# Three of the first seven weight tiles move from one load queue to the other

## The chip, the cores and the metric

The kernel runs on one core of one Trainium2 chip. The metric is the device time of one execution in microseconds (us). The engines are TensorE (PE in the rows, with PEld for its weight loads), VectorE (DVE), ScalarE (ACT), GpSimd (POOL) and SyncE (SP). SP, ScalarE and GpSimd each issue DMAs on a queue of their own; in the rows these issues stand as SPq, ACTq and POOLq.

## The reference

Two layers of a relational graph attention network over 3125 nodes of 768 features, 53125 edges and 3 relations, then a residual sum and a layer norm:

```python
xr = jnp.einsum('nd,rdf->rnf', x, W)          # W: 3 x 768 x 768
qi = xr[etype, dst] @ q; kj = xr[etype, src] @ k
alpha = leaky_relu(qi + kj, 0.2)
a = segment_softmax(alpha, dst)               # by destination node
out = segment_sum(a[:, :, None] * oj.reshape(-1, heads, out_ch), dst) + b
...
h = elu(layer(x, W1, q1, k1, b1)); out = layer(h, W2, q2, k2, b2)
return layernorm(x + out)
```

The first layer has four heads, the second one. The edges are sorted by destination.

## The kernel before, in words

The kernel has a preparation, which takes some 120 us, and three phases, which take the rest. Every matmul of fp32 data is made of a high part (a cast) and a low part (the difference); that is what the names H and L stand for (`wH`, `wL`, `tH`, `tL`).

The order of the work is written out by hand: within the manual schedule each engine does its instructions in the order in which the Python code issues them.

The preparation goes through the 18 tiles of W1, each 128 rows of 768 values (384 KB), two at a time. In `weights_kq`, `turn(m)` transposes tiles 2m and 2m+1 on TensorE (line 263), ScalarE makes the high part of each tile (line 303), VectorE or GpSimd the low part (line 304; VectorE for every third tile), ScalarE and VectorE split the transposed tiles (lines 273 and 274). `product` multiplies them by k and q (line 285), `place` writes the result into `wk` (lines 319 to 325). After `turn(m)` come `product(m-1)` and `place(m-2)`.

The tiles come in by `Buffers`: seven buffers of the tile `share` are filled at once, and each one that is freed (after its low part) takes the next tile of the list, W1's first, then x's blocks. All these loads stand on SP's queue (lines 178 and 181).

Beside the weights runs `prepare`, a generator of which `more(1)` does one step after each group. Its first step loads the three edge arrays dst, src and edge type as 125 rows of 425 int32 values (line 191, ScalarE's queue). Its second step scales dst on VectorE (line 208), stores it to a DRAM array `ed_d` (line 205) and fills the margins of `ed_d` and `dr_d` with constants, in four small-grained stores (lines 211 and 212); all five stores stand on GpSimd's queue, ahead of the low parts that GpSimd makes. A later step joins src and edge type (line 216, VectorE).

The tile framework deals out eight completion semaphores in turn to the loads of SP's and ScalarE's queues, in the order of the program. An issue whose semaphore still belongs to a load under way waits for that load.

Of the kernel before, what the change touches and what calls it, by code (L numbers as in the profile page):

```python
# [20 lines left out]
P = 128  # L21
# [33 lines left out]
def kernel(  # L55
# [19 lines left out]
    nc = tc.nc  # L75
# [7 lines left out]
    l1, l2 = layers  # L83
# [67 lines left out]
    class Buffers:  # L151
# [20 lines left out]
        def go(self):  # L172
            while self.waiting and self.spare:
                key = self.waiting.pop(0)
                self.at[key] = self.spare.pop(0)
                kind, i = key
                if kind == "W":
                    nc.sync.dma_start(self[key], l1["W"].rearrange("r (t p) f -> (r t) p f", p=P)[i])
                elif kind == "x":
                    n = min(P, N - i * P)  # L180
                    nc.sync.dma_start(self[key][:n], x[i * P:i * P + n, :])
# [305 lines left out]
    def a_load(pre, b):  # L487
        s = a_st[b] = {}
        r0 = start(b, regs)
        s["T"] = pre.tile([3 * (SL + 1), P], F32, name="T", bufs=2)  # L490
        nc.sync.dma_start(s["T"], at(ed_d, 0, 0, [[LL, 3], [P, SL + 1], [1, P]], r0))
# [755 lines left out]
    with tc.manual_schedule():  # L1247
        with tc.tile_pool(name="share", bufs=1) as pool:
            share = [pool.tile([P, RW], F32, name=f"share{i}") for i in range(9)]

            two = pall.rearrange("p b j h -> p (b j h)")
            xbs = [t[:, :D] for t in share] + [two[:, i * D:(i + 1) * D] for i in range(2)]
            with tc.tile_pool(name="wbuf", bufs=1) as wbuf:
                wH = wbuf.tile([P, R * DT, D + 2], F32R, name="wH")
                wL = wbuf.tile([P, R * DT, D + 2], F32R, name="wL")
                with tc.tile_pool(name="pre", bufs=1) as pre:
                    qq = pre.tile([P, NB, H1, R], F32, name="qq")
                    with tc.tile_pool(name="work0", bufs=1) as work, tc.tile_pool(
                        name="psum0", bufs=1, space=PSUM
                    ) as psum:  # L1260

                        bank = psum.tile([P, 512], F32, name="bank")
                        bits = prepare(work, bank, share[8], share[6].bitcast(BF))

                        def more(n):
                            for _ in range(n):
                                next(bits, None)

                        buf = Buffers()
                        buf.go()  # L1270
                        kqr = work.tile([P, DT, 2, H1], F32, name="kqr", bufs=1)
                        for s, name in ((0, "k"), (1, "q")):
                            nc.scalar.dma_start(kqr[:, :, s, :], l1[name].rearrange("(t p) h -> p t h", p=P))
                        more(1)
                        wk, kqs = (work.tile([P, DT, P], F32R, name=n) for n in ("wk", "kqs"))

                        def edges_ready():
                            more(100)
                            a_load(pre, 0)

                        turns = nodes_kq(buf, pre, work, psum, bank, wk, kqs, wH, wL, qq, more, edges_ready)
                        weights_kq(buf, work, psum, bank, kqr, wk, kqs, wH, wL, next(turns), more)
                        next(turns)
                    with tc.tile_pool(name="work1", bufs=1) as work, tc.tile_pool(
                        name="psum1", bufs=1, space=PSUM
                    ) as psum:
                        phase1(pre, work, psum, wH, wL, qq)
                with tc.tile_pool(name="work2", bufs=1) as work, tc.tile_pool(name="psum2", bufs=1, space=PSUM) as psum:
                    phase2(work, psum, wH, wL)
            with tc.tile_pool(name="work3", bufs=1) as work, tc.tile_pool(name="psum3", bufs=1, space=PSUM) as psum:  # L1290
                phase3(work, psum)
# [538 lines left out]
```

## Time and profile before

| | us |
|---|---|
| median of 3 runs | 2750.47 |
| lowest and highest | 2748.6, 2752.66 |
| the profiled execution's own time | 2741.27 |
| its span | 2739.5 |
| TensorE busy | 2054.5 (75%) |
| GpSimd busy | 1322.5 (48%) |
| VectorE busy | 1195.6 (44%) |
| ScalarE busy | 369.7 (13%) |

The rows of the profile come from one execution. Its times are counted from the start of the span; the execution's own time lies a little above the span, and this execution was some 9 us faster than the median of the timed runs. A row of the timeline has the start, the length, the engine, the line, the operation, what is written and read, and in brackets how long the engine was idle before it and what released it. Line numbers are those of the kernel before.

### The profile page before, as it was taken

The page shows a single profiled execution, that of the slowest core. Times are in us where ns is not written, and L with a number is a line of the kernel's source. Part 1 is how long each engine was busy: PE and PEld are TensorE (multiplying, and loading weights), DVE is VectorE, ACT ScalarE, POOL GpSimd, SP SyncE. Part 2 cuts the span into 40 slices and gives each one's busy share as a digit, 9 for nine tenths or more (in the row PEclk, how much of TensorE's full clock was granted, in tenths as well). Part 3 has the DMA queues.
Part 4 walks back from the last instruction along what each step waited for, and adds up shares of the span by engine and source line. Part 5 has one row for each costly group of instructions (what it writes and reads, how often), then busy time and mean ns, then how long its engine had stood idle before and what let it go on. Part 6 is the DMA issues. An engine that isn't in the chain of part 4 may idle for free.

```text
span 2739.5 us, 41906 instructions
## 1 busy us (share of the span) xinstructions
PE 2054.5 (75%) x15027; PEld 1606.6 (59%) x15027; DVE 1195.6 (44%) x4159; ACT 369.7 (13%) x658; POOL 1322.5 (48%) x1326
## 2 busy tenths in 40 slices
PE   7867888777776767888888898889936566565655
PEld 6756676667665645777677777767723232333323
DVE  6423333333332245445544554455424545444444
ACT  5301111111111000101110111111100111111111
POOL 3355555454543454444444434443255656566561
PEclk9967888888887878999999999999966777676777
DMA  7533333333332467666665656665577888877781
GB/s 193 142 95 120 114 114 114 113 106 115 103 108 99 143 213 244 198 201 203 203 200 187 214 185 211 192 212 191 175 271 246 272 267 267 276 253 259 251 262 61
DMA packets 156844, 506.31 MB, mean 185 GB/s; under 512 B 43875, under 2 KB 57069, under 8 KB 156628
## 3 DMA queue, kind: packets, MB, share of 16 engines
q0 software_dynamic: 81904, 331.52, 39.8%
q1 hardware_dynamic: 62926, 156.02, 16.1%
q10 hardware_dynamic: 11798, 16.00, 1.9%
q8 instruction: 122, 2.00, 0.3%
q14 instruction: 94, 0.77, 0.1%
HBM read 412.55 MB, written 95.69 MB: 186 GB/s over the span
## 4 chain that ended last, share of the span: by engine, by line
PE 52%; issue 17%; another core or an unknown queue 12%; DVE 11%; POOL 3%; DMA 3%; ACT 1%; POOLq 0%; ACTq 0%; DVEq 0%; SPq 0%
PE po L931 15%; PE po L698 14%; PE acc L875 9%; PE acc L1126 8%; DVE selp L853 3%; POOL G L462 2%; DMA G<-ftab,ridx 1%; PE bank L285 1%; DVE y L888 1%; PE bc L1033 1%; PE pt L263 1%; PE pt L906 1%; PE po L395 1%; DVE selp L1112 1%
## 5 line engine op out<-in xcount | busy, mean ns | idle before, releaser
L462 POOL DMA_INDIRECT kt<-kt,ridx x374 | 393.6, 1052 | 387.7 <-DVE lim L557 266.3
L698 PE MATMUL po<-wH,xT 128*128 128x384 f32 x1584 | 498.5, 382 | 107.5 <-issue 67.0
L931 PE MATMUL po<-wH,hT 128*128 128x386 f32 (+1 forms) x1800 | 514.7, 361 | 31.7 <-issue 27.3
L462 POOL DMA_INDIRECT G<-ftab,ridx x374 | 372.9, 997 | 242.2 <-PE acc L1126 110.4
L1126 PE MATMUL acc<-G,selp 128*32 128x386 f32 x2488 | 343.2, 621 | 102.6 <-DVE selp L1112 79.9
L698 PEld LDWEIGHTS po<-wH,xT 128*128 128x128 f32 x1584 | 331.2, 215 | 145.0 <-issue 92.0
L931 PEld LDWEIGHTS po<-wH,hT 128*128 128x128 f32 x1800 | 353.0, 202 | 67.3 <-issue 61.9
L853 DVE TENSOR_SCALAR selp<-frow,fdl,pall 128x32 f32<-128x32 f32 (+1 forms) x1688 | 380.3, 309 | 20.1 <-remote 17.3
L462 POOL DMA_INDIRECT share<-ftab,ridx x239 | 238.4, 997 | 299.7 <-PE acc L875 223.4
L931 PE MATMUL po<-wL,hT 128*128 128x386 f32 (+1 forms) x900 | 321.9, 358 | 14.4 <-issue 14.4
L698 PE MATMUL po<-wL,xT 128*128 128x384 f32 x792 | 296.2, 374 | 36.3 <-issue 35.8
L1126 PEld LDWEIGHTS acc<-G,selp 128*32 128x32 f32 x2488 | 190.6, 132 | 217.4 <-DVE selp L1112 107.0
L875 PE MATMUL acc<-share,selp 128*32 128x193 f32 x3208 | 229.6, 335 | 35.0 <-issue 31.4
L462 POOL DMA_INDIRECT g<-ftab,ridx x135 | 134.7, 998 | 191.9 <-PE acc L875 146.5
L698 PEld LDWEIGHTS po<-wL,xT 128*128 128x128 f32 x792 | 170.3, 215 | 48.3 <-issue 48.1
L875 PEld LDWEIGHTS acc<-share,selp 128*32 128x32 f32 x3208 | 131.0, 111 | 107.7 <-issue 77.5
L931 PEld LDWEIGHTS po<-wL,hT 128*128 128x128 f32 x900 | 182.4, 203 | 17.7 <-issue 17.4
L939 ACT COPY r<-po 128x386 f32<-128x386 f32 (+1 forms) x150 | 72.2, 481 | 834.5 <-PE po L931 621.4
L875 PE MATMUL acc<-g,selp 128*32 128x193 f32 x1768 | 139.4, 332 | 18.6 <-issue 15.7
L713 ACT COPY share<-po 128x384 f32<-128x384 f32 x144 | 67.1, 478 | 594.3 <-remote 260.6
L943 DVE COPY q<-po 128x1 f32<-128x1 f32 x75 | 11.6, 155 | 275.8 <-ACT r L939 275.7
L1039 DVE TENSOR_SCALAR sT<-bc,cols 128x512 bf16<-128x512 f32 (+1 forms) x125 | 83.4, 668 | 108.1 <-PE bc L1033 87.4
(245 smaller groups left out, 1986.0 us busy)
## 6 DMA issues: line engine op xcount, KB each, us to landing
ftab<-share SPq DMA_DIRECT2D x75, 386.0 KB
ftab<-r SPq DMA_DIRECT2D x75, 386.0 KB
share<-in_L_gnn_W_dram SPq DMA_DIRECT2D x36, 384.0 KB
w_d<-w2hl SPq DMA_DIRECT2D x18, 768.0 KB
sT<-dr_d SPq DMA_DIRECT2D x25, 544.0 KB
share<-in_x_dram SPq DMA_DIRECT2D x25, 384.0 KB
xb_d<-share SPq DMA_DIRECT2D x25, 384.0 KB
xr<-in_x_dram SPq DMA_DIRECT2D x23, 384.0 KB
```

The lines of the kernel that those rows point to most:

```text
L263: T.transpose(pt[:, f, c * P:(c + 1) * P], a[:, (2 * i + f) * P:(2 * i + f + 1) * P], ident)
L285: T.matmul(to, a[:, 2 * i + f, :], t[:, f, :w], start=(n == 0), stop=(n == 2 * DT - 1))
L395: T.matmul(po[g][:, :HALF], a[:, t % 2, :], w[:, r * DT + t, c * HALF:(c + 1) * HALF], start=(t == 0 and n == 0), stop=(t == DT - 1 and n ...
L462: return G.indirect_dma_start(out=to, out_offset=None, in_=tab, in_offset=_index(i[:, j:j + 1]), bounds_check=NP * R - 1, oob_is_err=False)
L698: m = T.matmul(po[:, :HALF], xT[:, s, t, :], w[:, i, sl], start=(n == 0), stop=(n == 3 * DT - 1))
L713: S.copy(to, po[:, :HALF].rearrange("p (h f) -> p h f", h=2))
L853: V.tensor_scalar(sel[:, h, :hi - lo], row[:, lo:hi], dl[:, b, j:j + 1], pall[:, b, j, h:h + 1], op0=ALU.is_equal, op1=ALU.mult)
L875: T.matmul(acc[32 * t:32 * t + 32, h // 2, c], sel[:, h, 32 * (t - WINDOW[i][0]):][:, :32], g[:, h * CW:(h + 1) * CW], start=(i == u[0] an ...
L931: T.matmul(po[:, :wd], hT[:, k, t, :], w[:, r * DT + t, sl], start=(t == 0 and n == 0), stop=(t == DT - 1 and n == 2))
L939: S.copy(o[:, c * HW:c * HW + wd], po[:, :wd])
L1039: V.tensor_scalar(s["sT"][:, 4 * i * P:4 * i * P + n], bc[:, :n], cols[:, b:b + 1], None, op0=ALU.is_equal)
L1126: T.matmul(acc[32 * t:32 * t + 32, c, :HW], st[b, j][:, 32 * (t - WINDOW[j][0]):][:, :32], gs[:, (base(b) + j) % NG, c * HW:(c + 1) * HW], ...
```

## The change

Tiles 1, 3 and 5 of W1 are issued on ScalarE's queue; all others stay with SP. `buf.go()`, which issues the first seven tiles, moves behind the issues of k and q. So on ScalarE's queue the order is k, q, three tiles, dst, src, edge type.

```diff
                 if kind == "W":
-                    nc.sync.dma_start(self[key], l1["W"].rearrange("r (t p) f -> (r t) p f", p=P)[i])
+                    (nc.scalar if i in (1, 3, 5) else nc.sync).dma_start(self[key], l1["W"].rearrange("r (t p) f -> (r t) p f", p=P)[i])
...
                         buf = Buffers()
-                        buf.go()
                         kqr = work.tile([P, DT, 2, H1], F32, name="kqr", bufs=1)
                         for s, name in ((0, "k"), (1, "q")):
                             nc.scalar.dma_start(kqr[:, :, s, :], l1[name].rearrange("(t p) h -> p t h", p=P))
+                        buf.go()
                         more(1)
```

The order on SP's queue before, from the program's start. The tiles `share_104` to `share_109` and `share_111` are the seven buffers; `DMAHW0` to `DMAHW7` are the completion semaphores of the loads from SP and ScalarE:

```order
L178 DMA share_104<-in_L_gnn_W_dram 128x768
L178 DMA share_105<-in_L_gnn_W_dram 128x768
L178 DMA share_106<-in_L_gnn_W_dram 128x768
L178 DMA share_107<-in_L_gnn_W_dram 128x768 [waits DMAHW0_49]
L178 DMA share_108<-in_L_gnn_W_dram 128x768 [waits DMAHW1_49]
L178 DMA share_109<-in_L_gnn_W_dram 128x768 [waits DMAHW2_49]
L178 DMA share_111<-in_L_gnn_W_dram 128x768 [waits DMAHW3_49]
L178 DMA share_104<-in_L_gnn_W_dram 128x768 [waits DMAHW4_49,PE_49,Pool_49]
L178 DMA share_105<-in_L_gnn_W_dram 128x768 [waits DMAHW5_49,PE_49,Pool_49]
L178 DMA share_106<-in_L_gnn_W_dram 128x768 [waits DMAHW6_49,DMAHW7_49,DVE_49,PE_49]
```

And with the change, the same place:

```order
L178 DMA share_104<-in_L_gnn_W_dram 128x768
L178 DMA share_106<-in_L_gnn_W_dram 128x768
L178 DMA share_108<-in_L_gnn_W_dram 128x768
L178 DMA share_111<-in_L_gnn_W_dram 128x768 [waits DMAHW0_49]
L178 DMA share_104<-in_L_gnn_W_dram 128x768 [waits DMAHW1_49,DMAHW4_49,PE_49,Pool_49]
L178 DMA share_105<-in_L_gnn_W_dram 128x768 [waits DMAHW3_49,DMAHW5_49,PE_49,Pool_49]
L178 DMA share_106<-in_L_gnn_W_dram 128x768 [waits DMAHW6_49,DVE_49,PE_49]
```

Before, the seventh tile (`share_111`) waited for DMAHW3, which was dst's, and the tenth (the second `share_106`) for DMAHW6, which was the edge type's. Now the seventh waits for DMAHW0, which is k's, and the tenth for the fifth tile's. The eighth (the second `share_104`) needs GpSimd's and TensorE's work on the first tile in both.

The head of ScalarE's queue before:

```order
L1273 DMA kqr<-in_L_gnn_k_dram 128x6x4
L1273 DMA kqr<-in_L_gnn_q_dram 128x6x4
L191 DMA e<-in_dst_dram 125x425
L191 DMA e<-in_src_dram 125x425
L191 DMA e<-in_edge_type_dram 125x425
L303 ACT_TABLE_LOAD
```

And with the change:

```order
L1272 DMA kqr<-in_L_gnn_k_dram 128x6x4
L1272 DMA kqr<-in_L_gnn_q_dram 128x6x4
L178 DMA share_105<-in_L_gnn_W_dram 128x768
L178 DMA share_107<-in_L_gnn_W_dram 128x768
L178 DMA share_109<-in_L_gnn_W_dram 128x768
L191 DMA e<-in_dst_dram 125x425 [waits DMAHW1_49]
L191 DMA e<-in_src_dram 125x425 [waits DMAHW2_49]
L191 DMA e<-in_edge_type_dram 125x425 [waits DMAHW3_49]
L303 ACT_TABLE_LOAD
```

The three edge arrays stand behind three tiles now, and each waits for a semaphore at its issue: dst for the first tile's, src for q's, edge type for the second tile's. TensorE's, VectorE's and GpSimd's instructions stand in the same order as before.

## The prediction

> **What bounds the kernel now.** I read the page first: its span and the shares of the chain that ended last.
>
> ```profile
> span 2739.5 us, 41906 instructions
> ...
> PE 52%; issue 17%; another core or an unknown queue 12%; DVE 11%; POOL 3%; DMA 3%; ACT 1%; POOLq 0%; ACTq 0%; DVEq 0%; SPq 0%
> ```
>
> TensorE carries the kernel, but the edit lies in the first few microseconds, so the second view is that chain for the opening stretch alone (start, length, what).
>
> ```profile
> 1.83 8.65 DMA e<-in_dst_dram
> ...
> 11.21 0.77 POOL ed_d L205
> ...
> 14.63 3.37 POOL wL L304 x2
> 18.02 7.73 DMA share<-in_L_gnn_W_dram
> 25.75 0.05 DVE e L216
> ...
> 29.13 3.78 DVE w L323
> ...
> 35.16 0.44 PE pt L263 x2
> ...
> 116.43 0.33 PE pt L371 x2
> ```
>
> Up to 35 us the chain hops over loads, GpSimd and VectorE; from 35.16 to 116.43 us it is TensorE work with no load in it. So whatever the change adds or saves before 35 us is carried to the end. The third view is the waits of TensorE and of SP's queue, in total, times and longest; the last two rows are of the stretch from 12 to 30 us.
>
> ```profile
> PE pt L263 <- DMA share<-in_L_gnn_W_dram: 13.8, 5, 4.4
> ...
> SPq L178 <- DMA e<-in_dst_dram: 3.6, 1, 3.6
> SPq L178 <- DMA kqr<-in_L_gnn_k_dram: 2.5, 1, 2.5
> ...
> SPq L178 <- POOL wL L304: 9.1, 3, 5.6
> SPq L178 <- DMA e<-in_edge_type_dram: 7.3, 1, 7.3
> ```
>
> TensorE waits five times for W1, and never after 27 us. SP waits for loads of the other queue, because eight completion semaphores (DMAHW0 to 7) are dealt out in turn to both queues and one is reused only when its last load has landed. The fourth view is the timeline around the last two of those five waits.
>
> ```profile
> 0.74 0.88 SPq L178 DMA_DIRECT2D share<-in_L_gnn_W_dram  x2
> 4.59 0.33 SPq L178 DMA_DIRECT2D share<-in_L_gnn_W_dram  x1
> 10.50 0.33 SPq L178 DMA_DIRECT2D share<-in_L_gnn_W_dram  x1
> 16.51 0.33 SPq L178 DMA_DIRECT2D share<-in_L_gnn_W_dram  x1
> 25.77 0.33 SPq L178 DMA_DIRECT2D share<-in_L_gnn_W_dram  x1
> ...
> 4.39 0.45 PE L263 MATMUL pt<-fident,share 128*128 128x128 f32 x1 [4.39 <-DMA share<-in_L_gnn_W_dram]
> 24.37 0.45 PE L263 MATMUL pt<-fident,share 128*128 128x128 f32 x1 [3.77 <-DMA share<-in_L_gnn_W_dram]
> 26.45 2.61 PE L263 MATMUL pt<-fident,share 128*128 128x128 f32 x11 [1.64 <-DMA share<-in_L_gnn_W_dram]
> ```
>
> I number the tiles W0 to W17. W6 is issued at 10.50, when dst has landed; W7 at 16.51, when GpSimd has finished W0's low part; W9 at 25.77, when the edge types have landed. TensorE gets W6 at 24.37 and W7 at 26.45. W0, issued at 0.74, feeds TensorE 3.65 us later, at 4.39; W7 takes 9.94. The table by stretches says why (us, PE, PEld, DVE, ACT and POOL busy, clock, DMA share, GB/s).
>
> ```profile
> 5.00:10.50 5.50, 2.82 (x12) 2.42 (x12) 1.10 (x3) 4.40 (x7) 0.00 (x0) 1.00 1.01 278
> 10.50:14.50 4.00, 2.88 (x14) 2.88 (x15) 3.99 (x8) 2.24 (x4) 3.29 (x5) 1.00 0.76 235
> 17.00:23.50 6.50, 2.72 (x24) 2.42 (x21) 0.00 (x0) 3.25 (x7) 2.49 (x2) 0.98 0.75 40
> 27.00:37.10 10.10, 8.66 (x54) 7.12 (x52) 9.89 (x18) 6.32 (x14) 6.49 (x7) 0.85 0.88 278
> ```
>
> From 17.0 to 23.5 us the engines are 75% busy and move 40 GB/s: each packet hangs. The stretch follows directly on GpSimd's stores of the margins, which by the code are 1,280 pieces of 4 to 80 bytes:
>
> ```profile
> 10.51 0.38 DVE L208 TENSOR_SCALAR e<-e 125x425 f32<-125x425 int32 x1 [2.65 <-DMA e<-in_dst_dram]
> 11.21 0.77 POOL L205 DMA_DIRECT2D ed_d<-e  x1 [9.64 <-DVE cols L129]
> ...
> 14.08 0.54 POOL L212 DMA_DIRECT2D dr_d<-padb  x1
> 14.63 4.86 POOL L304 TENSOR_TENSOR wL<-share,wH 128x768 fp32r<-128x768 f32 x3
> ```
>
> So the order is: dst lands, VectorE scales it, GpSimd issues five stores, then works W0's low part, then W7 may be loaded, into the stretch in which stores hold the DMA engines. That those stores cause the stretch is inferred from its place; no row names it.
>
> **The change part by part.** W1, W3 and W5 leave SP's queue. SP issues W0, W2, W4 without a wait and W6 after k alone, which is what W3 waited for until 4.59. SP no longer stands behind dst for W6 or behind the edge types for W9. Three issues of 0.33 us leave SP. The Trainium skill (DMA: Bandwidth & Descriptors, section "Issuing engines are not separate DMA queues") says that loads from several engines run on the same 16 DMA engines and interleave, and that only issue time is saved. By that rule the whole gain would be 3 x 0.33 = 1.0 us of SP's time; no run here shows it yet. SP is not late for want of issue time, so I count nothing for it.
>
> W6's earlier arrival alone is worth nothing: its group needs W7 too, and W7 still hangs on GpSimd. That cover is 26.45 - 24.37 = 2.1 us; were W7 there first, W6 would count.
>
> On ScalarE's queue the three tiles stand between q and dst. This is the term that costs. The bytes ahead of dst: the seven tiles of 393 KB, 2.75 MB, as SP's four take turns with ScalarE's three. Up to 5.00 us 0.82 MB have moved, and dst, source and edge type go over few engines:
>
> ```profile
> DMA packets 1340, 0.82 MB, mean 164 GB/s; under 512 B 1079, under 2 KB 1079, under 8 KB 1340
> ...
> q10 hardware_dynamic: 1958, 0.66, 8.3%
> ```
>
> The second row is ScalarE's queue up to 60 us (packets, MB, share): 1,536 pieces of k and q and 375 rows of the three edge arrays leave 47 packets, which are the ends of five loads: 16 each for k and q, 15 for three, so five DMA engines each. Of the 0.82 MB some 0.80 are tiles. The other 1.95 MB at 278 GB/s take 7.0 us, to 12.0. Then dst, 0.2125 MB on five of sixteen engines, 87 GB/s: 2.4 us, to 14.4. VectorE used it at 10.51: dst comes 3.9 us later. Lower bound: one tile fewer ahead (1.4 us less) and dst at the full rate (1.6 less), 0.9 us. Upper: 235 GB/s throughout, 8.3 + 2.9, 16.2, 5.7 us. I take 3.9, since the row from 5.0 to 10.5 is the same mixture of loads.
>
> With dst go VectorE's L208, the five stores, W0's low part and W7's issue, from 16.51 to 20.4, and the stretch in which the stores hold the engines too. The 9.94 us from issue to use stay, so W7 feeds TensorE at 30.3 instead of 26.45: **+3.9**.
>
> ScalarE itself now waits three times at its issues (dst for W0, source for q, edge type for W1), and its table load and casts are queued behind the last. W1 must pass q and shares with W4: about 4.5 tiles, 1.77 MB, so 0.95 MB after 5.00, 8.4 us instead of 5.82.
>
> ```profile
> 5.82 2.82 PE L263 MATMUL pt<-fident,share 128*128 128x128 f32 x12 [0.98 <-DMA share<-in_L_gnn_W_dram]
> ...
> 4.17 1.28 ACT L303 ACT_TABLE_LOAD   x1 [4.17 <-issue]
> ...
> 19.89 0.36 ACT L313 COPY sm<-bank 16x256 f32<-16x256 f32 x1
> ```
>
> The table load goes from 4.17 to about 8.8, 4.6 us later, so ScalarE's copy at 19.89 comes at 24.5 at most. Who waits for it is TensorE's next group, which waits for W7 till 30.3: cost nothing; without that cover it would be up to 24.9 against 24.37.
>
> A saving follows. The edge types land before 20 us (14.4 plus two more such loads of 2.4) and not at 25.75, so VectorE's L216, its low parts and GpSimd's no longer pile up behind 25.75. Before, TensorE waited for that pile:
>
> ```profile
> 33.97 0.44 PE L263 MATMUL pt<-fident,share 128*128 128x128 f32 x2 [0.51 <-DVE tL L274]
> 34.57 0.44 PE L263 MATMUL pt<-fident,share 128*128 128x128 f32 x2 [0.16 <-DVE tL L274]
> 35.16 0.44 PE L263 MATMUL pt<-fident,share 128*128 128x128 f32 x2 [0.16 <-DVE tL L274]
> ```
>
> 0.51 + 0.16 + 0.16: **-0.8**. At worst 0, if the pile only moves. W8 to W13 follow W7 on SP and were never waited for. Sum: 3.9 - 0.8 = **+3.1 us**, with the bounds of dst from +0.1 (0.9 - 0.8) to +5.7.
>
> **The rivals.** *The stores hold longer (slower).* Before, five engines were behind with the edge arrays, so their margin stores came after the stretch; eleven made it. The row of GpSimd's queue from 23.5 to 26.5 us shows the rest, where no store had been issued since 14.08:
>
> ```profile
> q0 software_dynamic: 23, 0.01, 1.7%
> ```
>
>  With dst last in its ring all sixteen store together: 6.5 x 16/11 = 9.5 us, 3.0 more, +6.1 in all, 2756.6; with dst at its upper bound +7.9. It decides if TensorE gets W7 over 12 us after its issue. For it: 40 GB/s is saturation, which more writers don't relieve. Against: the same number of bytes is stored.
>
> *The stores don't hold W7 (faster).* The hold may come from the five late engines and not from the stores. Then W7 takes the 3.65 us of W0: 20.4 + 3.65 = 24.1, 2.4 earlier, with the 0.8 -3.2 us, 2747.3; with dst only 0.9 late, -6.2. For it: the edge loads are alone on those engines. Against: W7 has 128 rows like k and q and so uses all sixteen, and between 17.0 and 23.5 none moved much. The Trainium skill (the same page, section "Queues, rings and completion order") says that a load's completion count lands only after every earlier write of that DMA engine, across its queues; by this W7 would still be counted behind the margin stores. W6, issued at 10.50 and used at 24.37, agrees.
>
> *The shift is lost later.* Phase 1 is paced by gathers, and a start some us later could meet the clock's throttle otherwise. No row prices it; I give it little.
>
> **How the numbers follow.** The profiled execution took 2741.27 us (span 2739.5), 9.2 below the median of the runs, 2750.47; I add the sum to the median: 2750.5 + 3.1 = 2753.6. About 0.2%, 5.5 us, is what a measurement of this kernel can tell from no change. Chances: the forecast 0.42 (0.35 of it within 0.2%, 0.07 slower, as dst's upper bound), stores hold longer 0.37 (all slower), don't hold 0.16 (0.09 within, 0.07 faster), lost later 0.05 (0.04 faster, 0.01 slower). Faster 0.11, same 0.44, slower 0.45. The range reaches from 2746 (most of the third case) to 2760 (the second, with dst late): little more than 1 in 10 is outside.
>
> **What would show it.** Right: VectorE's L208 near 14.4, GpSimd's first low part near 18.5, W7's issue near 20.4, TensorE's last wait for W1 ending near 30.3, L216 before that, TensorE's 0.51 wait for tL gone. Wrong: L208 before 11.5 (dst is not held), or W7 in under 5 us after its issue (the stretch is not the stores'), or a low GB/s stretch of over 8 us (the second case).

## The result, and the profile after

The two kernels ran in turn on the same chip, twelve times each.

| | before | after |
|---|---|---|
| median of 12 runs | 2751.99 us (2744.03 to 2762.7) | 2750.49 us (2741.97 to 2754.28) |
| ratio, 95% interval | 1 | 0.9991, 0.9977 to 1.0005 |
| profiled execution, its span | 2741.27 us, 2739.5 | 2750.36 us, 2748.6 |

The interval holds 1, so no movement is told from none. The two profiled executions are 9.1 us apart the wrong way round; that is scatter of single executions (the runs of one kernel spread over 12 to 19 us). What the change itself does must therefore be read in the preparation, the first 117 us, and there two marks do it: TensorE's last wait for W1 and its first instruction of phase 1 (L541).

The page of after, its span and the chain that ended last:

```profile
span 2748.6 us, 41909 instructions
...
PE 48%; issue 13%; DVE 10%; another core or an unknown queue 9%; DMA 1%; POOL 1%; ACT 1%; POOLq 0%; DVEq 0%; ACTq 0%; SPq 0%
```

TensorE still carries the kernel. The timeline of after, at the places that the prediction named (start, busy time, then what it is, and in brackets the idle time before it):

```profile
8.31 4.31 PE L263 MATMUL pt<-fident,share 128*128 128x128 f32 x23 [3.25 <-DMA share<-in_L_gnn_W_dram]
8.58 1.28 ACT L303 ACT_TABLE_LOAD   x1 [8.58 <-DMA share<-in_L_gnn_W_dram]
12.58 0.38 DVE L208 TENSOR_SCALAR e<-e 125x425 f32<-125x425 int32 x1 [4.63 <-DMA e<-in_dst_dram]
13.28 0.77 POOL L205 DMA_DIRECT2D ed_d<-e  x1 [11.71 <-DVE cols L129]
16.70 4.86 POOL L304 TENSOR_TENSOR wL<-share,wH 128x768 fp32r<-128x768 f32 x3
17.39 4.63 DVE L216 SCALAR_TENSOR_TENSOR e<-e 125x425 f32<-125x425 int32 x1
18.58 0.33 SPq L178 DMA_DIRECT2D share<-in_L_gnn_W_dram  x1
26.99 2.61 PE L263 MATMUL pt<-fident,share 128*128 128x128 f32 x11 [7.19 <-DMA share<-in_L_gnn_W_dram]
```

And its stretches, the four that the prediction showed of before (busy us of PE, PEld, DVE, ACT and POOL, clock, DMA share, GB/s):

```profile
5.00:10.50 5.50, 2.25 (x12) 2.20 (x12) 1.09 (x3) 1.91 (x2) 0.00 (x0) 1.00 1.01 366
10.50:14.50 4.00, 3.18 (x22) 2.91 (x22) 1.92 (x5) 4.00 (x8) 1.22 (x2) 1.00 0.34 125
17.00:23.50 6.50, 1.66 (x13) 1.24 (x11) 6.50 (x5) 2.92 (x6) 5.72 (x5) 0.87 0.61 32
27.00:37.10 10.10, 9.20 (x57) 8.67 (x57) 6.06 (x14) 7.21 (x15) 4.42 (x4) 0.75 0.95 330
```

Up to W7's issue the preparation keeps its shape, moved by 2 us: dst lands and is scaled at 12.58, the stores go out from 13.28 (11.21 before), W7 is issued at 18.58 into a stretch that moves 32 GB/s, and TensorE gets it at 26.99. What differs is the first row: 366 GB/s where before had 278.

The end of the preparation, on TensorE, first of before, then of after:

```profile
117.12 0.26 PE L541 MATMUL pT<-fident,T 54*128 54x54 f32 x1 [0.37 <-ACT g L373]
```

```profile
116.28 0.27 PE L541 MATMUL pT<-fident,T 54*128 54x54 f32 x1 [0.37 <-ACT g L373]
```

Phase 1 starts 0.84 us **earlier**, where the forecast had it 3.1 later. The table holds the steps; each number is a row above or in the prediction, or the difference of two. A second profile of after (e8 below) has its mark at 116.35; before was profiled once, so how far its 117.12 scatters is not known.

| step | before | after | moved | forecast |
|---|---|---|---|---|
| VectorE scales dst (L208) | 10.51 | 12.58 | +2.07 | +3.9 |
| W7's issue | 16.51 | 18.58 | +2.07 | +3.9 |
| from W7's issue to its use | 9.94 | 8.41 | -1.53 | 0 |
| from W7's use to L541 | 90.67 | 89.29 | -1.38 | -0.8 |
| L541 | 117.12 | 116.28 | **-0.84** | +3.1 |

### The profile page after: what moved, and what is told of

Read it like the earlier page. It is cut to its first block, busy times and chain, and to the rows that moved or that the text cites. A ratio compares the mean times of both kernels' runs of the same rounds, so it can differ in the third digit from the quotient of the medians.

```text
span 2748.6 us, 41909 instructions
## 1 busy us (share of the span) xinstructions
PE 2063.6 (75%) x15027; PEld 1606.4 (58%) x15027; DVE 1197.7 (44%) x4159; ACT 369.6 (13%) x658; POOL 1321.9 (48%) x1326
## 4 chain that ended last, share of the span: by engine, by line
PE 48%; issue 13%; DVE 10%; another core or an unknown queue 9%; DMA 1%; POOL 1%; ACT 1%; POOLq 0%; DVEq 0%; ACTq 0%; SPq 0%
PE po L931 15%; PE po L698 12%; PE acc L875 9%; PE acc L1126 8%; DVE selp L853 2%; PE bc L1033 1%; DVE y L888 1%; PE pt L906 1%; DVE selp L1112 1%; DVE ey L899 1%; DVE stats L1169 1%; DVE sT L1039 1%; PE px L675 1%; POOL G L462 1%
## 5 line engine op out<-in xcount | busy, mean ns | idle before, releaser
L698 PE MATMUL po<-wH,xT 128*128 128x384 f32 x1584 | 505.1, 385 | 105.5 <-issue 84.0
```

Source lines behind the costliest of these rows:

```text
L698: m = T.matmul(po[:, :HALF], xT[:, s, t, :], w[:, i, sl], start=(n == 0), stop=(n == 3 * DT - 1))
```

## The experiments

The theory going in: dst behind three tiles delays the margin stores and W7, and the stores hold W7. The rival: the hold is of something else, or what counts is where k, q and W1 stand. In e1 to e4, each run once side by side with before (2756.16 us there), the mark L541 decides and not the time.

**Coarser margins, on after (e1) and on before (e2).** The margins are written in 256 pieces of 16 to 640 bytes, not in 1,280 of 4 to 80; the bytes are the same.

```diff
-pad = work.tile([P, 4, BACK // P], F32, name="pad")
-padb = work.tile([P, BACK // P], BF, name="padb")
-front = work.tile([P, 4, FRONT // P], F32, name="front")
+pad = work.tile([16, 4, BACK // 16], F32, name="pad")
+padb = work.tile([32, BACK // 32], BF, name="padb")
+front = work.tile([32, 4, FRONT // 32], F32, name="front")
...
-for a, lo_, n in ((front, 0, FRONT), (pad, FRONT + E, BACK)):
-    G.dma_start(ed_d[:, lo_:lo_ + n].rearrange("r (p k) -> p r k", p=P), a)
-    G.dma_start(dr_d[0, lo_:lo_ + n].rearrange("(p k) -> p k", p=P), padb[:, :n // P])
+for a, lo_, n, w in ((front, 0, FRONT, 32), (pad, FRONT + E, BACK, 16)):
+    G.dma_start(ed_d[:, lo_:lo_ + n].rearrange("r (p k) -> p r k", p=w), a)
+    G.dma_start(dr_d[0, lo_:lo_ + n].rearrange("(p k) -> p k", p=32), padb[:, :n // 32])
```

> The changed kernel with the margins stored in 256 pieces of 16 to 640 bytes instead of 1,280 of 4 to 80 bytes (same bytes, same place in the queue). Theory 'stores': the low-rate stretch (17.0 to 23.5 us and on) is made by the small stores and holds W7. Then dst's L208 stays near 12.6 and W7's issue near 18.6, but W7 is used 3.7 to 5 us later (22.2 to 23.6 instead of 26.99) and the preparation's end (phase 1's first TensorE instruction, L541, at 116.28 in the changed kernel) moves to 111.5 to 112.9. Rival 'five engines': the stretch comes from the three edge arrays that run on five DMA engines; then W7 is used near 27 and L541 stands near 116.3.

> The kernel before with the same coarser margin stores. Theory 'stores': W7's issue stays near 16.5 and W7 is used near 20.2 to 21.5 instead of 26.45; L541 moves from 117.12 to 111 to 112. Then dst's earlier place is worth something only without the hold, and the kernel before would be level with the changed one or ahead of it. Rival 'five engines': W7 used near 26.4, L541 near 117.1.

Measured: e1 2750.08 us, L541 at 113.52; e2 2734.11 us, L541 at 109.96. The timeline and two stretches of e1:

```profile
12.41 0.39 DVE L208 TENSOR_SCALAR e<-e 125x425 f32<-125x425 int32 x1 [4.70 <-DMA e<-in_dst_dram]
16.02 4.87 POOL L304 TENSOR_TENSOR wL<-share,wH 128x768 fp32r<-128x768 f32 x3
17.23 4.13 DVE L216 SCALAR_TENSOR_TENSOR e<-e 125x425 f32<-125x425 int32 x1
17.92 0.33 SPq L178 DMA_DIRECT2D share<-in_L_gnn_W_dram  x1
21.12 1.48 PE L263 MATMUL pt<-fident,share 128*128 128x128 f32 x11 [1.39 <-DMA share<-in_L_gnn_W_dram]
24.17 0.80 PE L285 MATMUL bank<-tH,kqs 128*128 128x256 f32 x2 [1.57 <-DVE g L321]
113.52 0.26 PE L541 MATMUL pT<-fident,T 54*128 54x54 f32 x1 [0.37 <-ACT g L373]
17.00:23.50 6.50, 2.98 (x22) 2.26 (x21) 6.50 (x6) 5.16 (x10) 5.72 (x5) 0.91 0.58 171
27.00:37.10 10.10, 9.20 (x56) 8.82 (x56) 9.74 (x22) 7.81 (x15) 4.76 (x4) 0.72 0.88 278
```

And of e2, with its first stretch too:

```profile
9.72 0.38 DVE L208 TENSOR_SCALAR e<-e 125x425 f32<-125x425 int32 x1 [1.95 <-DMA e<-in_dst_dram]
18.58 0.60 DVE L216 SCALAR_TENSOR_TENSOR e<-e 125x425 f32<-125x425 int32 x1 [2.61 <-DMA e<-in_edge_type_dram]
20.91 1.53 PE L263 MATMUL pt<-fident,share 128*128 128x128 f32 x12
22.20 0.48 PE L285 MATMUL bank<-tH,kqs 128*128 128x256 f32 x2
109.96 0.26 PE L541 MATMUL pT<-fident,T 54*128 54x54 f32 x1 [0.37 <-ACT g L373]
5.00:10.50 5.50, 2.82 (x12) 2.42 (x12) 1.88 (x6) 4.34 (x7) 0.08 (x1) 1.00 1.02 278
17.00:23.50 6.50, 5.61 (x50) 5.38 (x49) 4.89 (x7) 6.40 (x12) 5.18 (x5) 1.00 0.85 268
27.00:37.10 10.10, 8.88 (x66) 7.65 (x66) 9.49 (x25) 6.79 (x15) 3.88 (x3) 1.00 0.81 261
```

The hold is that of the small stores, which the prediction had only inferred from its place: with 256 pieces the stretch moves 171 and 268 GB/s, and W7 takes 3.20 us (17.92 to 21.12) instead of 8.41. The third case of the prediction, that the stores do not hold W7, falls.

But with the hold gone the order of the two kernels turns: e1 reaches phase 1 3.56 us after e2. Both marks miss what was expected, e1 later (111.5 to 112.9 was expected, though W7 came sooner than expected) and e2 earlier (111 to 112). The rows show two things in e1 that e2 does not have.

The first is a wait that the prediction does not have. L216 starts at 17.23, while GpSimd works its three low parts (16.02 to 20.89), and takes 4.13 us where it takes 0.60 in e2. TensorE then waits 1.57 us for g, which VectorE does behind it, and starts its product at 24.17, 1.97 us behind e2's 22.20. In after the same 4.63 us of L216 lie behind TensorE's wait for W7, and cost nothing.

The second is TensorE's granted clock. From 27.0 to 37.1 us it is 0.72 in e1 and 1.00 in e2, and from 23.5 to 27.0 it is 0.50 and 1.00. The pairs of the product at L285 follow each other after 0.43 us in e1 and after 0.24 in e2, and by the next product e1 is 3.42 us behind (31.63 and 28.21). So about half of the 3.56 us stands with the wait and half with the clock. Why the clock fell in e1 and not in e2, no run separates.

**Only the queue, not the place (e4).** `buf.go()` goes back ahead of k and q, and the three tiles stay on ScalarE's queue.

```diff
 buf = Buffers()
+buf.go()
 kqr = work.tile([P, DT, 2, H1], F32, name="kqr", bufs=1)
 ...
-buf.go()
 more(1)
```

> Only the first edit: tiles 1, 3 and 5 on ScalarE's queue, buf.go() left ahead of k and q, so that the tiles run ahead of k and q. Theory 'bytes ahead of dst': the same bytes stand ahead of dst, so L208 is near 12.6 (12 to 13.5), W7 used near 27, L541 near 116.3 (within 0.7). Rival 'k and q late': k and q come behind three tiles, the products wait for them and L541 is over 1 us later.

```profile
11.17 0.19 DVE L293 CAST kqs<-kqr 128x48 fp32r<-128x48 f32 x1 [9.10 <-DMA kqr<-in_L_gnn_q_dram]
12.84 0.38 DVE L208 TENSOR_SCALAR e<-e 125x425 f32<-125x425 int32 x1 [0.42 <-DMA e<-in_dst_dram]
28.72 2.61 PE L263 MATMUL pt<-fident,share 128*128 128x128 f32 x11 [7.44 <-DMA share<-in_L_gnn_W_dram]
118.02 0.26 PE L541 MATMUL pT<-fident,T 54*128 54x54 f32 x1 [0.37 <-ACT g L373]
```

Measured: 2758.91 us. L208 comes at 12.84, within 0.26 us of after: what counts for dst are the bytes ahead of it, not their order. q lands behind the tiles and is cast at 11.17, where after has 6.71. The end is 1.74 us after that of after, but the rows do not lay this on q. TensorE gets W7 1.73 us later (28.72 and 26.99), and from there to L541 both take the same, 89.30 and 89.29. W7 was issued only 0.28 us later (18.86 and 18.58), so from issue to use it took 9.86 us here and 8.41 in after; why, is not known. The expectation's rival had the size right, over 1 us, but not the way: no product waits for k and q. What it is worth to have k and q first, no run shows.

**The tiles behind the edge arrays (e3).** `buf.go()` moves to the other side of `more(1)`.

```diff
-buf.go()
 more(1)
+buf.go()
```

> The changed kernel with ScalarE's three tiles behind the edge arrays instead of ahead of them (k, q, dst, source, edge type, W1, W3, W5). Theory 'dst sets W7': L208 near 9 to 10.5 instead of 12.58, W7's issue six us later (15 to 16.5), its use 8.4 to 9.9 after that (23.5 to 26.4), L541 1 to 3 us before 116.28. Rival 'W1 binds': W1 behind three edge arrays lands after 12 us, the first groups come so late that L541 stands at 116.3 or later in spite of W7.

```profile
9.50 0.38 DVE L208 TENSOR_SCALAR e<-e 125x425 f32<-125x425 int32 x1 [1.83 <-DMA e<-in_dst_dram]
20.89 4.60 PE L263 MATMUL pt<-fident,share 128*128 128x128 f32 x23 [15.91 <-DMA share<-in_L_gnn_W_dram]
119.61 0.26 PE L541 MATMUL pT<-fident,T 54*128 54x54 f32 x1 [0.37 <-ACT g L373]
17.00:23.50 6.50, 2.61 (x12) 2.42 (x12) 0.88 (x2) 2.01 (x3) 1.55 (x1) 1.00 0.22 31
```

Measured: 2759.81 us, as the expectation's rival had it. dst is early again, 9.50, so its lateness in after is that of the three tiles ahead of it. But now W1 itself is not through when the stretch begins (31 GB/s): TensorE waits 15.91 us for it, and phase 1 starts 3.33 us later than in after. Early stores are no gain in themselves; whatever stands behind them in time pays.

**L216 one step later (e5).** To take the new wait out of e1, one more `yield` stands ahead of L216's step (lines below it are one higher). e5 to e8 ran on another chip, where before takes 2054.76 us (median of 15); their times are compared with that alone.

```diff
 yield
 yield
+yield
 rx = tile_(F32)
```

> The changed kernel with coarser margins, and the step with L216 (source and edge type) one group later. In the run with coarser margins alone L216 took 4.13 us, until GpSimd's three low parts were done, and L541 stood at 113.52 instead of the 109.96 of the kernel before with coarser margins. Theory 'L216 meets the low parts': moved away it takes 0.6 us, and L541 falls to 111 to 112. Rival 'whatever VectorE reads from SBUF there is held': VectorE's own low part of W5, which comes next, takes over 3 us in its place and L541 stays within 0.4 of 113.5.

```profile
15.84 6.65 POOL L305 TENSOR_TENSOR wL<-share,wH 128x768 fp32r<-128x768 f32 x4
17.24 6.08 DVE L305 TENSOR_TENSOR wL<-share,wH 128x768 fp32r<-128x768 f32 x1
25.26 0.80 PE L286 MATMUL bank<-tH,kqs 128*128 128x256 f32 x2 [3.00 <-DVE g L322]
25.76 0.60 DVE L217 SCALAR_TENSOR_TENSOR e<-e 125x425 f32<-125x425 int32 x1
114.25 0.26 PE L542 MATMUL pT<-fident,T 54*128 54x54 f32 x1 [0.37 <-ACT g L374]
```

Measured: 2050.70 us, one execution; phase 1 starts no earlier (114.25 against 113.52 and, on this chip, 113.86). L216 is back at 0.60 us, and VectorE's own low part is held instead, 6.08 us: it starts at 17.24, inside GpSimd's four, and ends at 23.32, 0.83 us after them. So the wait belongs to what VectorE starts with both operands in SBUF in that time, and not to L216. The clock fell here too, to 0.70 from 27.0 to 37.1 us, and so this run does not tell the wait's share from the clock's either.

**The three versions timed (e6: before with coarser margins; e7: after with them; e8: after alone).** Kernels as above.

> The kernel before with coarser margins, timed. Its preparation ended 7.2 us earlier in one profile (L541 at 109.96 instead of 117.12). If what the preparation saves is carried to the end, the ratio is 1 - 7.2/2750 = 0.9974, with an interval that lies below 1; if later stages give it back, the ratio is within 0.001 of 1.

> The changed kernel with coarser margins, timed. L541 stood at 113.52, 3.6 us before the kernel before and 3.6 after the kernel before with coarser margins: a ratio of 0.9987 if the preparation's gain is carried, and above that of the kernel before with coarser margins by 0.0013. If the queue change were good in itself it would be the faster of the two.

> The changed kernel as it is, timed beside the others on the same chip. L541 stood 0.84 us earlier than before: a ratio of 0.9997, not to be told from 1; a ratio below 0.998 or above 1.002 would mean that something behind the preparation moves too.

| | median, runs | ratio to before, 95% | L541 | 117.12 less that, of 2054.76 |
|---|---|---|---|---|
| e6 | 2045.42, 5 | 0.9953, 0.9940 to 0.9967 | 109.63 | 7.49 us, 0.9964 |
| e7 | 2047.52, 5 | 0.9957, 0.9943 to 0.9970 | 113.86 | 3.26 us, 0.9984 |
| e8 | 2052.06, 11 | 0.9989, 0.9980 to 0.9998 | 116.35 | 0.77 us, 0.9996 |

The mark carries over between the chips: e6, e7 and e8 have L541 within 0.35 us of e2, e1 and after, so the chips differ behind the preparation. Before itself was not profiled on this chip, so its 117.12 is that of the first. e6 and e7 are faster than was expected (0.9974 and 0.9987). What the mark says of the time lies within the intervals of e6 and e8, and outside that of e7, which is faster than its preparation explains. e8 says that the change is a shade faster, by 0.02 to 0.20%; the twelve pairs on the other chip could not tell. Of its 2.7 us the preparation shows 0.8; where the rest of e7 and e8 comes from was not found, so it stays open. Before with coarser margins (e6) has the lowest median, but its interval and e7's cover nearly the same values, so the times do not rank the two; their marks do, by 4.23 us.

## Why the prediction came out as it did

The time, 2750.49 us, lies in the range, and no difference can be told, as most of the forecast's case had it. That says little for the sum, as the range of 14 us holds no change at all as well. The +3.1 us is not what happened, and that the time fits is in part luck: the step that costs was forecast too large, and two others, W7's wait and the saving on VectorE, came out in the kernel's favour.

**Early W1, table load: right, W1 in part by luck.** TensorE's first long wait ends at 8.31 (8.4 said), though after moved 1.27 MB from 5.0 to 8.3 us, at 386 GB/s, where the prediction had 0.95 MB at 278. The two misses cancel. ScalarE's table load starts at 8.58 (8.8 said), and nothing waits for it: TensorE waits for W7 till 26.99.

**dst: the direction right, the size wrong.** The mis-sized term is "1.95 MB at 278 GB/s". That rate was read from a row in which the edge arrays ran beside the tiles. With the change they do not. ScalarE's queue from 5.0 to 10.5 us, of after (packets, MB, share):

```profile
q10 hardware_dynamic: 779, 1.24, 62.0%
```

Its three tiles are 1.18 MB, so that is nearly all it did in that time. By after's own row 1.95 MB at 366 GB/s take 5.3 us, to 10.3, and with the prediction's 2.4 us for dst 12.7; L208 stands at 12.58. That sum comes out a little too well: from 10.5 to 14.5 us, with edge arrays almost alone, after moved 125 GB/s, not the 87 that the 2.4 us rest on, and dst at 125 would be through at 12.0. The 0.6 us from there to L208 are not explained.

The runs go one way. Where the edge arrays run beside the tiles, the stretch has 278 (before, e2), 280 (e3) and 283 GB/s (e6); where they come behind all of them, 366 to 370 (after, e1, e5, e7, e8). In e4, where the tiles are through sooner, it has 416 up to 9.0 us and 100 from there to 10.5. The row was the same stretch of time but not, as the prediction had it, "the same mixture of loads".

The +2.07 lies within the bounds, 0.9 and 5.7. The margins come behind dst, so two more pairs measure the same delay: e1 less e2 gives 12.41 - 9.72 = 2.69 us, e7 less e6 12.79 - 9.45 = 3.34. All three stay below 3.9, and before's 10.51 is the latest of the three profiles with the old order.

**W7's 9.94 us: "stay" was wrong, and why is only in part known.** The stores hold W7, as said, and the end of the hold moved with them. The traffic from 23.5 to 26.5 us in 40 slices (GB/s), of before:

```profile
GB/s 146 23 244 180 241 86 123 127 132 150 109 314 373 369 350 355 459 391 227 451 369 246 369 164 410 205 123 246 123 82 164 41 123 123 41 164 82 41 41 82
```

And of after, with the only queue that has packets in that time:

```profile
GB/s 0 41 0 82 123 82 41 123 82 82 82 0 123 41 123 164 82 82 164 82 123 123 82 123 0 123 41 123 82 0 41 0 41 41 41 369 369 328 410 328
q1 hardware_dynamic: 119, 0.33, 70.4%
```

In before the rate climbs over 300 GB/s at 24.3 us, in after at 26.1: 1.8 us later, nearly the 2.07 of the stores. What shrank is the rest. In after TensorE has W7 0.9 us behind the climb, in before 2.1 us, and in before the rate fell once more in between. In this window before still carried 33 packets of ScalarE's queue and 23 of GpSimd's; in after only SP's loads (q1) are left. That the five engines with the edge arrays were the ones behind, and no longer are, fits, but no run separates it. Nor is the size firm: e8, the same kernel as after, took 9.04 us from W7's issue to its use (18.26 to 27.30), and e4 9.86.

**VectorE's pile: right, and worth more.** The three waits for tL are gone. TensorE's rows of before and of after, from the group behind W7's to its product (the pairs at 33.97 to 35.16 stand in the prediction):

```profile
29.52 3.34 POOL L304 TENSOR_TENSOR wL<-share,wH 128x768 fp32r<-128x768 f32 x2
31.93 1.53 PE L263 MATMUL pt<-fident,share 128*128 128x128 f32 x12
35.36 0.48 PE L285 MATMUL bank<-tH,kqs 128*128 128x256 f32 x2
```

```profile
32.84 2.18 PE L263 MATMUL pt<-fident,share 128*128 128x128 f32 x18
33.24 0.18 DVE L323 TENSOR_TENSOR w<-g 128x16 f32<-128x16 f32 x1
34.78 0.49 PE L285 MATMUL bank<-tH,kqs 128*128 128x256 f32 x2
```

Before, 18 transposes and their product's start took 35.36 - 31.93 = 3.43 us; after, 34.78 - 32.84 = 1.94: -1.49. The waits were 0.83 of it. Most of the rest is that pairs take 0.44 us, 0.22 for one, and the unbroken run 2.18 / 18 = 0.12: 3 x (0.44 - 0.24) = 0.6. So here the waits that cut the run cost more than their idle time. The cause of the pile is the same hold as in e5: L323 took 3.78 us beside GpSimd's 3.34, and 0.18 now. Against it stand +0.37 from W7's use to 32.84 (the clock was 0.75 in this stretch and 0.85 before), and -0.26 behind 34.78: in all 0.37 - 1.49 - 0.26 = -1.38.

**The rivals.** "Don't hold W7" is refuted by e1 and e2. "Hold longer" did not come as it was priced: W7 was used 8.41 us after its issue and not over 12, and the climb came 1.8 us later where this rival has the stores' delay and 3.0 more. One of its signs did show, a low stretch of over 8 us: after stays at 32 GB/s from 17.0 to 23.5 and below 170 up to 26.1. But until W7's issue at 18.58 there was nothing to load, so the sign could not tell the cases apart. "The shift is lost later" could not be seen: 0.8 us are within the scatter of the profiled executions. What none of them had is the hold of VectorE by GpSimd, which is hidden in after and costs in e1, beside the clock.

## What to carry to other kernels

A transfer rate belongs to the mixture that ran in its row: before using it for a changed order, ask what still runs beside it. A delay ahead of a shared obstacle, here a burst of small stores, is not simply added to the end: dst's 2.07 us were 0.54 at W7's use (26.45 and 26.99). Find the obstacle first, since taking it away (e2, e6) brought phase 1 forward by 7 us where the change brought 0.84. When a wait is removed, look which engine's work has moved beside which other's: a step that was free in one order can stand for 4 us in the next. And before a wait is charged with a difference between two runs, compare their granted clocks.

## What was not expected of the hardware

Small stores held the loads out of all proportion to their bytes: 1,280 pieces of 4 to 80 bytes, some 50 KB in all, kept the loads at 32 to 40 GB/s for 6.5 us, and the same bytes in 256 pieces of 16 to 640 left 171 to 268 GB/s. Whether the number of pieces or their size does it, the runs do not separate, as both change.

VectorE's instructions with both operands in SBUF stand while GpSimd works a run of its low parts: L216 took 4.63 and 4.13 us for 0.60, a low part 6.08 for 0.95, L323 3.78 for 0.18. Its subtraction from PSUM does not, as these rows of after show:

```profile
30.25 0.69 DVE L274 TENSOR_TENSOR tL<-pt,tH 128x512 fp32r<-128x512 f32 x1 [0.16 <-ACT tH L273]
34.91 1.88 DVE L274 TENSOR_TENSOR tL<-pt,tH 128x512 fp32r<-128x512 f32 x3
34.97 1.56 POOL L304 TENSOR_TENSOR wL<-share,wH 128x768 fp32r<-128x768 f32 x1
```

Three took 1.88 us, 0.63 each, beside GpSimd for the most part; one with no GpSimd beside it takes 0.69 (at 30.25). The Trainium skill (SBUF — State Buffer, section "Who interferes with whom") says that a VectorE instruction with two SBUF inputs contends with a GpSimd instruction that reads SBUF, and that one with at most one SBUF input, outside the modes that use two ports, does not. The traces agree, and add the size: the hold lasted over several GpSimd instructions, 4.63 us where one of them takes 4.86 / 3 = 1.62. One cast with a single SBUF input was held as well: L324 in e1 at 35.12, 1.69 us for 0.17, beside a low part of GpSimd from 34.95 to 36.78. Whether it ran in such a mode, no row tells.
